# The tail of a graph-attention kernel: moments a slot sooner, scores ahead of the next product, two totals written together, the last quad whole

## The chip, the cores and the metric

The kernel runs on one core of one Trainium2 chip. The metric is the device time of an execution in microseconds (us); lower is better. Engines are named as in the profile: PE is TensorE (PEld its weight loads), DVE is VectorE, ACT is ScalarE, POOL is GpSimd, SP is SyncE, whose queue issues most DMAs. Before the change three runs took 2006.64, 2006.75 and 2006.97 us, a median of 2006.75.

## The reference, cut to what matters

A graph with 6250 nodes of 128 features and 206,250 edges, sorted by receiver. Each edge gets a weight vector from two small networks, a score per head (8 heads of 16), and a message; a node sums the messages that it receives, adds its own features and is normalized.

```
w     = silu(edge_a @ rad_W1 + b) @ rad_W2 + b  +  silu(edge_b @ sph_W1 + b) @ sph_W2 + b
alpha = sum over a head of (q[receiver] * w * k[sender]) / sqrt(16) * edge_weight
out   = segment_sum(alpha * v[sender], receiver) / 16
y     = layernorm(x + out)
```

Here q, k and v are the node features times Wq, Wk, Wv.

## The kernel before, in words

**Tiles.** 128 edges are a tile, 4 tiles a quad (512 edges), 4 quads a group (2048 edges). There are 403 quads in NG = 101 groups, numbered 0 to 100; the last group has three quads, which the tail calls a = 400, b = 402 and c = 401 (within a group the order of the quads is 0, 2, 1, 3). A first stage makes a table of k and v rows in DRAM. Then the loop runs over the groups, with four slots in each, one for a quad.

**One quad.** GpSimd gathers the k and v rows of its senders from the table, one gather for a tile (`gather`, line 127), into one of 16 buffers, 14 quads ahead of use. TensorE computes the first layers (`first_layers`, L472), ScalarE their silu (L502), TensorE the receivers' q at the edges by a one-hot product (`q_at_edges`, L481) and the weights w (`weigh`, L512 and L517). VectorE then does five steps: `multiply` (L526, q times k; needs the gather and L481), and in `scores` the product with w (L534), the sum over a head (L536), the scaling (L538), and in `messages` the product with v (L551). The messages are summed by TensorE into 32 rows a quad (`sum_quads`, L563).

**One group.** `part_sums` (L592) copies a group's sums out of PSUM on ScalarE. `sum_group` (L597, L599) places them, by one-hot matrices that `place` makes on VectorE (L586, L587), into a window of 128 nodes and adds what the window before left there; a copy on ScalarE (L601) gives the total `tot` of the group. `moments` (L613, L615, L616) adds the node features and computes mean and variance on VectorE; `roots` (L621) takes the square root on ScalarE; `normalize` computes a reciprocal and a shift on VectorE (L629, L631) and applies them on ScalarE (L635). `write_rows` (L647) writes a window's 128 rows (64 KB) to `out` from the SP queue. Windows of neighbouring groups overlap, so the later write to a row is the right one and a write to `out` waits for the one before it.

**Four groups at a time.** In the loop, `statistics` takes the moments of the group two before in slot 3, and normalizes when four groups are together. The last four, 97 to 100, are normalized in the tail, each by its own root and normalize: 97 first, then 98, 99 and 100.

**The tail** (lines 745 to 799). The three last quads have wide one-hots (`wide_one_hots`), so that `sum_wide` (L578) adds their messages straight into the last window, in PSUM, and `to_end` (L776) adds what group 99 left there. Before the change c is treated in two halves of two tiles: multiply, scores, messages and sums of a half, then of the other, with the normalize of 98 and the moments of 99 between them.

**The order of the work** is written out by hand: every engine runs its instructions in the order of the program, and semaphores are put in where one needs another's result. PSUM tiles have few buffers (`ph`, `pq`, `pw` two each, `po` one), so a product waits until the buffer's last reader is done. In the loop, `marks` are matmuls of the next quad's product: the helpers `after` and `behind` make an instruction on VectorE or ScalarE wait for one of them, so that it comes no sooner than this matmul; `mark` is the last matmul of `q_at_edges`.

Of the kernel before, what the change touches and what calls it, by code (L numbers as in the profile page):

```python
# [60 lines left out]
def gnn_kernel(ctx, tc, x, src, dst, weight, edges, rad_W1, rad_b1, rad_W2, rad_b2,  # L61
# [404 lines left out]
    with tc.tile_pool(name="ps", bufs=1, space=PSUM) as pp:  # L466
# [55 lines left out]
        def multiply(q, mark=None, t=slice(0, QT)):  # L522
            if t.start == 0:
                kq_of[q] = quad_of("kq", 3)
            for u, kv in kv_parts(q, t):
                o = nc.vector.tensor_tensor(kq_of[q][:, u, :], pq_of[q][:, u, :], kv[:, :, :D],  # L526
                                            op=OP.mult)
                if mark is not None:
                    after(o, mark)
# [15 lines left out]
        def messages(q, alpha, t=slice(0, QT), marks=()):  # L545

            if t.start == 0:
                msg_of[q] = quad_of("msg", XQ)
            for u, kv in kv_parts(q, t):
                n = u.stop - u.start  # L550
                o = nc.vector.tensor_tensor(  # L551
                    msg_of[q][:, u, :].rearrange("p t (h e) -> p t h e", e=HD),
                    kv[:, :, D:].rearrange("p t (h e) -> p t h e", e=HD),
                    alpha[:, u.start - t.start:u.stop - t.start, :, None].to_broadcast(
                        [P, n, HEADS, HD]), op=OP.mult)
                behind(o, marks, 3)
# [20 lines left out]
        def sum_wide(q, t, start=False, stop=False):  # L577
            nc.tensor.matmul(po_of[q // NQ], hot_of[q, "wide"][:, t, :], msg_of[q][:, t, :],  # L578
                             start=start, stop=stop)
# [9 lines left out]
        def part_sums(g):  # L589
            n = quads_in(g) * W  # L590
            part_of[g] = gp.tile([P, D], F32, name="part")
            nc.scalar.activation(part_of[g][:n, :], po_of[g][:n, :], AF.Copy)  # L592
# [46 lines left out]
        def statistics(g):  # L639
            moments(g, tot_of[g])  # L640
            if g < NG - LB and first_of(g + 1) > g:
                normalize(first_of(g), g + 1, roots(first_of(g), g + 1))
# [42 lines left out]
        for g in range(NG - 1):  # L685
            for slot, j in enumerate((0, 2, 1, 3)):
                q = g * NQ + j
                i = g * NQ + slot
                turned, past, old = None, mark, marks
                if slot == 0 and g == CHECK + len(checks) + 1:  # L690
                    verdict()
                if slot == 0:
                    turned = turn_q(g + 1, pp.tile([P, EQ], F32, name="pq", bufs=2))
                if slot == 1 and 2 <= g:
                    turned = sum_group(g - 2)
                if slot == 2:
                    turned = make_q(g + 1, pp.tile([P, EQ], F32, name="pq", bufs=2))
                if 1 <= g:
                    for t in ((), (0, 1), (2,), (3,))[slot]:
                        mark = sum_quads(g - 1, t)  # L700
                first_layers(order[i + 2])
                mark = q_at_edges(order[i + 1])
                marks = weigh(order[i + 1])
                silus(order[i + 2], mark, marks)
                if turned:
                    turned()
                if 1 <= g and slot == 3:
                    part_sums(g - 1)
                if i + AHEAD < len(order):
                    gathers(order[i + AHEAD], old[-QT:])  # L710
                multiply(order[i + 1], mark)
                messages(q, scores(q, marks=marks), marks=marks)
                if slot == 0:
                    if g + XL < NG:
                        load_x(g + XL, past)
                if slot == 2:
                    if g + 3 < NG:
                        load_feats(g + 3, past)
                    if g + 2 < NG:
                        load_rel(g + 2)  # L720
                if slot == 1:
                    one_hots_T(g + 1)
                    if g + 2 < NG:
                        pick(g + 2)
                    if 1 <= g:
                        place(g - 1)
                write_rows()
                load_rows(i)
                if slot == 3:
                    if 2 <= g:  # L730
                        statistics(g - 2)
                    if g + 1 < NG - 1:
                        one_hots(g + 1)
                    if CHECK <= g < CHECK + len(checks):
                        checks[g - CHECK]()
                if g == NG - 3 and slot in (0, 2):
                    wide_one_hots(order[slot // 2 - 3])
                if g == NG - 2 and slot == 0:
                    wide_one_hots(order[-1])
                    n = nc.values_load(general, min_val=0, max_val=1)  # L740
                if g == NG - 2 and slot == 2:
                    place(NG - 1)
                if g == NG - 2 and slot == 3:
                    place(g)
        g, (a, b, c) = NG - 1, order[-3:]
        halves = (slice(0, QT // 2), slice(QT // 2, QT))
# [1 line left out]
        mark = q_at_edges(b)  # L748
        marks = weigh(b)
        turned = sum_group(g - 2)  # L750
        for t in range(QT // 2):
            sum_quads(g - 1, t)
        silus(c, mark, marks)
        sd = roots(g - 3, g - 2)
        turned()
        multiply(b, mark)
        messages(a, scores(a, marks=marks), marks=marks)
        normalize(g - 3, g - 2, sd)
        write_rows()

        mark = q_at_edges(c)
        marks = weigh(c)
        for t in range(QT // 2, QT):
            sum_quads(g - 1, t)
        po_of[g] = pp.tile([P, EQ], F32, name="ph", bufs=2)[:, :D]
        for t in range(QT):
            sum_wide(a, t, start=(t == 0))
        part_sums(g - 1)
        turned = sum_group(g - 1)
        messages(b, scores(b, marks=marks), marks=marks)  # L770
        moments(g - 2, tot_of[g - 2])
        sd = roots(g - 2, g - 1)
        turned()
        for t in range(QT):
            sum_wide(b, t)
        nc.tensor.matmul(po_of[g], to_of[g][:, 1, :], tot_of[g - 1], start=False, stop=False)  # L776

        multiply(c, mark, halves[0])
        messages(c, scores(c, halves[0]), halves[0])
        for t in range(QT // 2):  # L780
            sum_wide(c, t)
        normalize(g - 2, g - 1, sd)
        write_rows()
        moments(g - 1, tot_of[g - 1])
        sd = roots(g - 1, g)
        multiply(c, mark, halves[1])
        messages(c, scores(c, halves[1]), halves[1])
        for t in range(QT // 2, QT):
            sum_wide(c, t, stop=(t == QT - 1))
        normalize(g - 1, g, sd)  # L790
        write_rows()
        moments(g, po_of[g])
        sd = roots(g, g + 1)
        rs = gp.tile([P, LB], F32, name="rs")
# [163 lines left out]
```

## Time and profile before

| | |
|---|---|
| median of three runs | 2006.75 us |
| profiled execution | 2007.43 us |
| its span, first to last instruction | 2005.3 us |
| PE busy | 1806.6 us (90%) |
| POOL busy | 1502.9 us (75%) |
| DVE busy | 1468.5 us (73%) |
| ACT busy | 718.5 us (36%) |
| last gather starts | 1987.24 us |
| last write of rows starts | 2000.85 us |

Times inside the profile are microseconds from the start of the span. The profiled execution took 2.13 us more than its span, and 0.68 us more than the median. A line of a view in order of time gives start, duration, engine, source line, operation, the tile written and the tiles read, shapes, and in brackets how long the engine sat idle before it and what ended that. VectorE starts an instruction a little before the one ahead of it has ended, so the steps between starts are what adds up. Busy time of PE counts overlapping matmuls and is not PE at its peak. A line of waits gives who waited, for whom, and then the total, the number of times and the longest.

The core's stages:

| us from the start | what runs | DVE busy |
|---|---|---|
| 0 to 55 | tables, node products, first gathers | 38.62 |
| 55 to 1988.2 | the loop and the start of the tail, gathers all along | 1420.19 |
| 1988.2 to 2000.85 | the rest of the tail | 9.67 |
| 2000.85 to 2005.3 | the last write and the end of the program | 0.00 |

### The profile page before, as it was taken

To read this page: it belongs to the slowest core of one execution; us is meant where nothing else is said; L and a number is where in the kernel's file an instruction comes from. 1 tells how busy PE (TensorE), PEld (TensorE's weight loads), DVE (VectorE), ACT (ScalarE), POOL (GpSimd) and SP (SyncE) were. 2 spreads that over 40 slices of the span, in tenths; PEclk is the share of its full clock that TensorE was granted. 3 is DMA by queue.
4 is the path that set the end of the run, shared out by engine and by line. 5 is a ranking of instruction groups with operands and counts; after the bars stand their busy time and mean duration, and the time that the engine had idled before them with its cause. 6 is when DMAs were issued, how large, how long until landed. Compare 5 with 4: busy or idle time off the path is not lost.

```text
span 2005.3 us, 51075 instructions
## 1 busy us (share of the span) xinstructions
PE 1806.6 (90%) x16012; PEld 1521.8 (76%) x16012; DVE 1468.5 (73%) x3087; ACT 718.5 (36%) x1426; POOL 1502.9 (75%) x1594
## 2 busy tenths in 40 slices
PE   9999999989899988989998899898988999888897
PEld 7788777867777767778877777777777777777776
DVE  6688787858787767777777676776767767767677
ACT  3244344424343333333333333342433333333333
POOL 7777777777777777777777777777777777777775
PEclk9899989988988988988888889898889888898898
DMA  8545555545555555555555555554455455455453
GB/s 313 158 141 153 149 150 152 157 142 153 154 144 152 155 144 153 154 144 151 155 145 153 147 147 152 144 156 140 141 155 154 143 150 156 142 151 144 139 154 86
DMA packets 146834, 304.50 MB, mean 152 GB/s; under 512 B 36940, under 2 KB 80060, under 8 KB 146556
## 3 DMA queue, kind: packets, MB, share of 16 engines
q0 software_dynamic: 75488, 205.36, 36.7%
q1 hardware_dynamic: 69568, 95.42, 14.6%
q8 instruction: 128, 2.10, 0.4%
q14 instruction: 150, 1.23, 0.2%
q10 hardware_dynamic: 1500, 0.40, 0.1%
HBM read 287.58 MB, written 13.46 MB: 150 GB/s over the span
## 4 chain that ended last, share of the span: by engine, by line
PE 61%; DMA 16%; DVE 9%; issue 5%; ACT 4%; POOL 3%; SPq 1%; DVEq 0%; POOLq 0%; ACTq 0%
PE pw L517 31%; DMA kv<-kv_tab,src_i 12%; PE pq L481 11%; PE ph L472 8%; PE po L563 4%; DVE kq L526 3%; DMA relb<-rel_lin 3%; PE pw L512 3%; POOL msg L127 2%; DVE kq L534 2%; ACT L502 2%; ACT y L635 1%; DVE side L536 1%; PE pq L212 1%; POOL kv L127 1%
## 5 line engine op out<-in xcount | busy, mean ns | idle before, releaser
L127 POOL DMA_INDIRECT kv<-kv_tab,src_i x1546 | 1463.0, 946 | 471.3 <-PE pw L517 182.9
L502 ACT ACTIVATE act<-ph,b 128x512 f32<-128x512 f32 x806 | 517.5, 685 | 1134.8 <-PE pq L481 1093.5
L517 PE MATMUL pw<-w,act 128*128 128x128 f32 x6448 | 914.8, 301 | 0.0
L517 PEld LDWEIGHTS pw<-w,act 128*128 128x128 f32 x6448 | 833.6, 209 | 105.8 <-issue 94.8
L481 PE MATMUL pq<-q,hotT 32*128 32x128 f32 x3224 | 505.5, 300 | 65.9 <-DVE hotT L218 43.0
L472 PE MATMUL ph<-feats,w 32*128 32x512 f32 x1612 | 502.3, 680 | 19.8 <-ACT act L502 19.0
L481 PEld LDWEIGHTS pq<-q,hotT 32*128 32x128 f32 x3224 | 424.8, 201 | 95.3 <-issue 57.7
L526 DVE TENSOR_TENSOR kq<-pq,kv 128x512 f32<-128x512 f32 (+1 forms) x404 | 273.8, 678 | 276.6 <-DMA kv<-kv_tab,src_i 122.2
L536 DVE TENSOR_REDUCE side<-kq 128x32 f32<-128x512 f32 x404 | 280.1, 693 | 42.8 <-DVE kq L534 0.9
L551 DVE TENSOR_TENSOR msg<-kv,side 128x512 f32<-128x512 f32 (+1 forms) x404 | 273.9, 678 | 42.9 <-DVE side L538 0.5
L534 DVE TENSOR_TENSOR kq<-pw,kq 128x512 f32<-128x512 f32 x404 | 274.5, 680 | 0.1
L472 PEld LDWEIGHTS ph<-feats,w 32*128 32x128 f32 x1612 | 136.8, 193 | 105.6 <-issue 60.5
L512 PE MATMUL pw<-brow,onesb 3*128 3x512 bf16 x403 | 162.5, 403 | 7.6 <-DVE kq L534 7.6
L563 PE MATMUL po<-msg,hot 128*32 128x128 f32 x3200 | 158.1, 295 | 0.0
L218 DVE TENSOR_TENSOR hotT<-relb,side 128x512 f32<-128x512 bf16 x101 | 68.9, 682 | 88.7 <-DMA relb<-rel_lin 88.7
L538 DVE TENSOR_TENSOR side<-side,scale 128x32 f32<-128x32 f32 x404 | 80.6, 200 | 42.6 <-DVE side L536 0.9
L597 PE MATMUL pq<-part,to 128*128 128x128 f32 x200 | 44.7, 307 | 68.9 <-DVE kq L526 46.7
L563 PEld LDWEIGHTS po<-msg,hot 128*32 128x32 f32 x3200 | 72.6, 113 | 39.6 <-issue 7.3
L597 PEld LDWEIGHTS pq<-part,to 128*128 128x128 f32 x200 | 31.8, 200 | 76.9 <-issue 43.9
L223 DVE TENSOR_TENSOR hot<-rel,side 128x512 f32<-128x512 f32 x100 | 66.2, 662 | 0.0
L212 PE MATMUL pq<-wq,xT 128*128 128x128 f32 x200 | 45.9, 316 | 18.6 <-DVE kq L526 18.5
L212 PEld LDWEIGHTS pq<-wq,xT 128*128 128x128 f32 x200 | 35.5, 222 | 21.8 <-DVE kq L526 21.4
(114 smaller groups left out, 849.6 us busy)
## 6 DMA issues: line engine op xcount, KB each, us to landing
wide<-kv_tab SPq DMA_DIRECT2D x3328, 1.0 KB
feats<-in_edges SPq DMA_DIRECT2D x101, 512.0 KB
kv<-kv_tab,src_i POOLq DMA_INDIRECT x1546
relb<-rel_lin SPq DMA_DIRECT2D x101, 128.0 KB
x<-in_x SPq DMA_DIRECT2D x101, 64.0 KB
out<-y SPq DMA_DIRECT2D x101, 64.0 KB
kv_tab<-kv SPq DMA_DIRECT2D x12, 512.0 KB
act<-in_x SPq DMA_DIRECT2D x12, 256.0 KB
```

Of the source, the lines that this page charges most:

```text
L127: return nc.gpsimd.indirect_dma_start(out=o, out_offset=None, in_=table, in_offset=bass.IndirectOffsetOnAxis(ap=index, axis=0))
L212: nc.tensor.matmul(pt[:n, :D], xT_of[g][:, :n], wq, start=True, stop=True)
L472: return nc.tensor.matmul(act_of[q, i], w1[r0:r0 + R, :], feats_of[g][r0:r0 + R, c0:c0 + EQ], start=True, stop=True)
L481: o = nc.tensor.matmul(pq_of[q][:, t, :], hotT_of[g][b, t * P:(t + 1) * P], q_of[g][b, :], start=True, stop=True)
L502: o = nc.scalar.activation(act, act_of[q, i], AF.Silu, bias=b1[:, i:i + 1])
L512: nc.tensor.matmul(pw, onesb, brow.rearrange("p t d -> p (t d)"), start=True, stop=False)
L517: o = nc.tensor.matmul(pw[:, t, :], act_of[q, i][:, t * P:(t + 1) * P], w2[:, i, :], start=False, stop=(t == QT - 1 and i == 1))
L526: o = nc.vector.tensor_tensor(kq_of[q][:, u, :], pq_of[q][:, u, :], kv[:, :, :D], op=OP.mult)
L534: nc.vector.tensor_tensor(m, pw_of[q][:, t, :], m, op=OP.mult)
L536: o = nc.vector.tensor_reduce(alpha, m.rearrange("p t (h e) -> p t h e", e=HD), AX.X, OP.add)
L551: o = nc.vector.tensor_tensor(msg_of[q][:, u, :].rearrange("p t (h e) -> p t h e", e=HD), kv[:, :, D:].rearrange("p t (h e) -> p t h e", e ...
L563: o = nc.tensor.matmul(po_of[g][j * W:(j + 1) * W, :], hot_of[g][:, j * QT + t, :], msg_of[g * NQ + j][:, t, :], start=(t == 0), stop=(t = ...
```

## The change

In the loop, `statistics` of group 97 and `place` of group 99 move from slot 3 of group 99 to slot 2. In the tail, a's scores and messages stand ahead of b's multiply, and the waits of scores and messages for `marks` are dropped; all of group 99's quads are summed in one place, its part is copied and its total summed ahead of c's product; the moments of 98 and 99 stand together, with one root and one normalize for both, and their rows are written one behind the other; c is multiplied and scored whole, and only its messages and their sums are in halves.

```diff
                 write_rows()
                 load_rows(i)
-                if slot == 3:
+                if slot == (3 if g < NG - 2 else 2):
                     if 2 <= g:
                         statistics(g - 2)
+                if slot == 3:
                     if g + 1 < NG - 1:
                         one_hots(g + 1)
...
                 if g == NG - 2 and slot == 2:
                     place(NG - 1)
-                if g == NG - 2 and slot == 3:
                     place(g)
...
         turned = sum_group(g - 2)
-        for t in range(QT // 2):
+        for t in range(QT):
             sum_quads(g - 1, t)
         silus(c, mark, marks)
         sd = roots(g - 3, g - 2)
         turned()
+        part_sums(g - 1)
+        messages(a, scores(a))
         multiply(b, mark)
-        messages(a, scores(a, marks=marks), marks=marks)
         normalize(g - 3, g - 2, sd)
         write_rows()
 
         mark = q_at_edges(c)
+        turned = sum_group(g - 1)
         marks = weigh(c)
-        for t in range(QT // 2, QT):
-            sum_quads(g - 1, t)
+        turned()
         po_of[g] = pp.tile([P, EQ], F32, name="ph", bufs=2)[:, :D]
         for t in range(QT):
             sum_wide(a, t, start=(t == 0))
-        part_sums(g - 1)
-        turned = sum_group(g - 1)
-        messages(b, scores(b, marks=marks), marks=marks)
-        moments(g - 2, tot_of[g - 2])
-        sd = roots(g - 2, g - 1)
-        turned()
+        nc.tensor.matmul(po_of[g], to_of[g][:, 1, :], tot_of[g - 1], start=False, stop=False)
+        messages(b, scores(b))
         for t in range(QT):
             sum_wide(b, t)
-        nc.tensor.matmul(po_of[g], to_of[g][:, 1, :], tot_of[g - 1], start=False, stop=False)
-
-        multiply(c, mark, halves[0])
-        messages(c, scores(c, halves[0]), halves[0])
-        for t in range(QT // 2):
-            sum_wide(c, t)
-        normalize(g - 2, g - 1, sd)
-        write_rows()
+        moments(g - 2, tot_of[g - 2])
         moments(g - 1, tot_of[g - 1])
-        sd = roots(g - 1, g)
-        multiply(c, mark, halves[1])
-        messages(c, scores(c, halves[1]), halves[1])
-        for t in range(QT // 2, QT):
-            sum_wide(c, t, stop=(t == QT - 1))
-        normalize(g - 1, g, sd)
-        write_rows()
+        sd = roots(g - 2, g)
+        multiply(c, mark)
+        normalize(g - 2, g, sd)
+        write_rows(2)
+        alpha = scores(c)
+        for h in halves:
+            messages(c, alpha[:, h], h)
+            for t in range(h.start, h.stop):
+                sum_wide(c, t, stop=(t == QT - 1))
         moments(g, po_of[g])
         sd = roots(g, g + 1)
```

## The prediction

> **What bounds the kernel now.** First view: the costliest groups of the page.
>
> ```profile
> L127 POOL DMA_INDIRECT kv<-kv_tab,src_i x1546 | 1463.0, 946 | 471.3 <-PE pw L517 182.9
> ```
>
> GpSimd issues 1546 gathers, each 0.946 us busy and 0.30 idle. 1546 x 1.25 = 1932 us, which is the whole stretch from the first kv gather to the last (1987.24). So up to about 1988 the gather queue sets the time, and the change leaves it alone: it can only alter what follows the last gathers. Second view: VectorE in order of time (start, duration, line, operation, tiles), from quad 397's messages to the end.
>
> ```profile
> 1979.30 0.69 DVE L551 TENSOR_TENSOR msg<-kv,side 128x512 f32<-128x512 f32 x1
> 1979.90 0.35 DVE L587 TENSOR_SCALAR to_end<-side,rowp 128x128 f32<-128x128 f32 x1
> 1980.41 0.69 DVE L526 TENSOR_TENSOR kq<-pq,kv 128x512 f32<-128x512 f32 x1 [0.16 <-PE pq L481]
> ...
> 1983.51 0.31 DVE L613 TENSOR_TENSOR y<-tot,x 128x128 f32<-128x128 f32 x1
> ...
> 1984.51 0.34 DVE L587 TENSOR_SCALAR to<-side,rowp 128x128 f32<-128x128 f32 x1
> 1985.60 0.69 DVE L526 TENSOR_TENSOR kq<-pq,kv 128x512 f32<-128x512 f32 x1 [0.75 <-DMA kv<-kv_tab,src_i]
> ...
> 1992.11 0.18 DVE L616 BATCH_NORM_AGGREGATE mv<-st 128x2 f32<-128x6 f32 x1
> 1992.21 0.41 DVE L526 TENSOR_TENSOR kq<-pq,kv 128x256 f32<-128x256 f32 x1
> ...
> 1995.23 0.40 DVE L526 TENSOR_TENSOR kq<-pq,kv 128x256 f32<-128x256 f32 x1
> ...
> 1996.80 0.42 DVE L551 TENSOR_TENSOR msg<-kv,side 128x256 f32<-128x256 f32 x1
> ...
> 1998.03 0.29 DVE L613 TENSOR_TENSOR y<-ph,x 128x128 f32<-128x128 f32 x1 [0.54 <-PE ph L578]
> ...
> 1999.48 0.35 DVE L798 TENSOR_SCALAR y<-y,mv,rs 128x128 f32<-128x128 f32 x1
> ```
>
> The reader is to see that VectorE waits once, 0.75 us for b's rows at 1985.60 (b = 402, c = 401, a = 400), and is then busy without a gap until c's second messages at 1996.80. The chain of waits puts 7.46 us on a gather before 1992.21, but that multiply starts 0.10 after the aggregate, as the one at 1995.23 does after its own: no wait. Third view: the last gather on GpSimd, the write queue, and its last long wait.
>
> ```profile
> 1987.24 0.95 POOL L127 DMA_INDIRECT kv<-kv_tab,src_i  x1 [0.30 <-issue]
> ...
> 1965.38 0.36 SPq L647 DMA_DIRECT2D out<-y  x1
> ...
> 1967.95 0.34 SPq L647 DMA_DIRECT2D out<-y  x1
> ...
> 1970.43 0.33 SPq L647 DMA_DIRECT2D out<-y  x1
> ...
> 1995.10 0.33 SPq L647 DMA_DIRECT2D out<-y  x1
> ...
> 1998.04 0.33 SPq L647 DMA_DIRECT2D out<-y  x1
> 2000.85 0.34 SPq L799 DMA_DIRECT2D out<-y  x1
> ```
>
> ```profile
> SPq L799 <- DMA out<-y: 2.4, 1, 2.4
> ```
>
> A write to out waits for the one before it. The last rows are ready at 1999.83 (1999.48 + 0.35), but their write starts at 2000.85, 2.81 after the write of group 99. From there 4.45 us follow to the end of the span.
>
> **The change part by part.** Steps on VectorE, start to start, from this execution: multiply 0.61; L534 0.79, L536 0.80, L538 0.30, L551 0.60 (one quad's scores and messages: 2.49); a group's moments 0.33 + 0.33 + 0.10 = 0.76; place 0.25 to 0.27 an instruction; reciprocal 0.19 and shift 0.08.
>
> *Moments of 97 and place of 99, a slot sooner.* Three and two VectorE instructions, no DMA (97 is not normalized there), no SP or GpSimd work. Their input, tot of 97, was copied by ScalarE at 1972.76, so they run at once. Messages of 397 at 1979.30, moments 1979.90, place(100) 1980.66, place(99) 1980.93 and 1981.20, multiply(a) 1981.45 instead of 1980.41. Behind multiply(a) on VectorE, L534 of 399 goes from 1981.02 to 1982.06; TensorE needs its buffer for the product of b (L512, 1983.43), so 0.7 us remain. The gathers no longer wait for this. In slot 3 the 1.3 us are missing, so b's rows (landed about 1985.5) would be waited for: the next part fills that.
>
> *Scores of a ahead of multiply(b).* L534(399) 1982.06, messages(399) 1983.95, L534(a) 1984.55 (its product was done at 1982.53), messages(a) 1986.44, multiply(b) 1987.04: no idle. The dropped waits for TensorE cost nothing seen: with them L536(a) followed L534(a) by 0.78, the same step as everywhere; I take 0, with 0.07 either way (the longest "issue" piece of this chain on VectorE).
> The price is that multiply(b) comes 1.44 later, and c's q at the edges waits for it on TensorE, with the sum of 99, c's product and the wide sums of a and b queued behind. L481 started 0.74 after such a multiply at 1960.16, so 1987.78; L481 to L517 takes 1.09 (1986.73 to 1987.82), the sum of 99 0.65 (1985.51 to 1986.16): c's product from 1989.52 to 1991.57.
>
> *All four sums of 99's quads at once.* The second sixteen matmuls, 0.57 to 0.65, run at 1986.7, needing messages(399) (done 1984.6). TensorE is idle from about 1987.3 to 1987.78. The copy of the part (0.28 on ScalarE) is then early; tot of 99 is copied near 1989.8, behind normalize(97) on ScalarE (shift 1987.84, done 1988.5). It used to land at 1992.8.
>
> *Both moments, one root, one normalize.* From multiply(b) 1987.04: reciprocal 1987.65, shift 1987.84, L534(b) 1987.92, messages(b) 1989.81, moments of 98 at 1990.41 and 99 at 1991.17, multiply(c) 1991.93. One root for two columns instead of two (ScalarE 0.29 less; 128x1 takes 0.294, 128x4 0.30). It is done about 1992.36, while multiply(c) runs: reciprocal 1992.54, shift 1992.73, L534(c) 1992.81, 1.2 us after c's product.
>
> *Last quad whole.* c's halves took 1.99 + 1.91 = 3.90; whole it takes 0.61 + 0.79 + 0.80 + 0.30 + 2 x 0.34 = 3.18. Six VectorE instructions fewer, 0.72 saved. Messages at 1994.70 and 1995.04. Then 1.23 to the last y (1996.80 to 1998.03), or up to 1.35 because eight matmuls run in a row (1.06 to 1.16 against 0.71 for four): I take 1.30, y at 1996.34. From y 1.80 to the end of L798: rows ready at 1998.14 instead of 1999.83, a gain of 1.69.
>
> *Two writes in a row.* The first copy by ScalarE (L635) starts 0.20 after shift and takes 0.49: rows of 98 at 1993.42, of 99 at 1993.8 (four in a row took 1.65). Write of 98 at 1993.45, write of 99 when that has landed, the last when 99 has. Back-to-back spacings in the trace: 2.57, 2.48 (two) and 2.81. I take 2.48 for the first and 2.81 for the second, which is the same pair at the same place: last write at 1998.74, 0.6 after its rows. Ends: 2 x 2.81 gives 1999.07; no wait gives 1998.17.
>
> Sum: last write from 2000.85 to 1998.74, 2.11 us sooner; ends 1.78 and 2.68. The 4.45 behind it stays. Against the profiled execution (span 2005.3, time 2007.43) that is 2005.3. The median of the runs shown is 0.68 below it, so I forecast 2006.75 - 2.11 = 2004.64.
>
> **A rule against the rows.** The Trainium skill, "DMA: Bandwidth & Descriptors", section "Anatomy of one DMA", has a fixed cost of about 2.0 us a DMA, most of it the write's receipt, plus bytes over 436 GB/s. By it 64 KB would take an estimated 2.15 us, two in a row would be over before the last rows are ready, and the time would be 2004.07. The row of 2.81, which holds issue, landing and wake-up, speaks for the longer one.
>
> **The rivals.**
> 1. *The writes don't bind.* If a write frees the next 2.3 us or less after its issue, the last write starts with its rows at 1998.17: gain 2.68, time 2004.07. For it: other waits of SP for out ended sooner after the issue (1.2 us). Against: all four back-to-back spacings are above 2.3. This is how the rule above would have it.
> 2. *TensorE's clock halves.* After idle gaps of 2.1 and 1.1 us (1964.04 to 1968.56) the granted clock was 0.50 from 1968.2 to 1974.7, and the sixteen matmuls of a product took 3.5 instead of 1.9. If that happened at 1987.78, c's product would end near 1994.4, L534(c) and all behind 1.6 later, the last write about 1999.8: gain 1.05, time 2005.7. Against: the gap there is 0.5 us.
> 3. *The gathers hold c.* Multiply(c) moves to 1991.93. The last gather starts at 1987.24; rows of earlier quads were there 2.7 to 3.2 us after the start, so 1990.5. Landing would have to take 4.7 us before it costs anything; at 5 us, the longest wait of multiply on a gather being 5.3, and the gain falls to 1.8: 2004.9.
> 4. *The other side: the write chain.* The change puts two landings ahead of the last write, starting at 1993.45, where before only that of 99, issued at 1998.04, lay at the end. At a spacing above 3.70 us (1993.45 + 2 x 3.70 = 2000.85) the kernel is slower than before; at 4.2 it takes 2007.75, and 0.2% slower takes 5.7. For it: the last wait was the longest in the tail. Against: no spacing above 2.81, and little other traffic after 1990 (mean 20 to 30 GB/s).
> 5. *It gains nothing* (2006.75): the order on VectorE would have to wait as much as it saves, for instance for tot of 99 (1.4 us to spare) or c's product (1.2).
>
> **How the numbers follow.** My sum 0.58, rival 1 0.20, rival 2 0.06, rival 3 0.06, rival 4 0.04, rival 5 0.06. The likeliest is 2004.64, with 2004.1 to 2005.0 of its own. For eight in ten I add about 0.5 below rival 1 for the landing of the last write (the queue waited 1.3 us for it), and above I reach past rival 2: 2003.6 to 2006.1. 0.2%, about 4.0 us, is what a measurement of this kernel can tell from no change. All but the extreme of rival 4 lie inside it; faster by 4.0 would need the last write at 1996.8, only 0.5 after the last y: 0.04. Slower by 4.0: 0.03, with what I have not thought of.
>
> **What would show it.** In the changed kernel's trace: L613 and L616 ahead of multiply(a), at about 1980; no wait for kv at b's multiply, about 1987.0; multiply(c) 128x512 near 1991.9; messages 128x256 twice within 0.4 us near 1995; two L647 writes 2.5 apart; L798 about 1997.8; L799's write within 0.6 us of its end. Wrong if the last gather shifts by more than 0.5 us, if VectorE waits for tensor work at L613 or L534, if the clock shows 0.50 near 1990, or if L799's wait is over 1 us.

## The result and the profile after

| | before | after |
|---|---|---|
| median of 18 runs each, one chip | 2006.94 us (2006.17 to 2008.00) | 2002.80 us (2002.29 to 2003.61) |
| ratio | | 0.998 (95%: 0.9972 to 0.9987) |
| profiled execution, its span | 2007.43, 2005.3 us | 2002.76, 2000.9 us |
| last gather starts | 1987.24 us | 1986.14 us |
| last rows ready | 1999.83 us | 1997.11 us |
| last write starts | 2000.85 us | 1997.14 us |
| last write to the end of the span | 4.45 us | 3.76 us |

The kernel gained 4.14 us, or 0.2%: little, but the interval of the ratio lies clear of 1. It is nearly twice the 2.11 us that I forecast. The time of 2002.80 us lies below the low end of my range (2003.6).

The page's costliest group is the same as before, as it should be: 1546 gathers, 0.946 us each.

```profile
L127 POOL DMA_INDIRECT kv<-kv_tab,src_i x1546 | 1462.4, 946 | 471.2 <-issue 192.6
```

VectorE of the changed kernel in order of time, from quad 397's messages to the end (start, duration, line, operation, tiles, idle time before it):

```profile
1978.86 0.69 DVE L551 TENSOR_TENSOR msg<-kv,side 128x512 f32<-128x512 f32 x1
1979.46 0.28 DVE L613 TENSOR_TENSOR y<-tot,x 128x128 f32<-128x128 f32 x1
...
1980.96 0.68 DVE L526 TENSOR_TENSOR kq<-pq,kv 128x512 f32<-128x512 f32 x1
...
1984.05 0.69 DVE L534 TENSOR_TENSOR kq<-pw,kq 128x512 f32<-128x512 f32 x1
1984.77 0.69 DVE L536 TENSOR_REDUCE side<-kq 128x32 f32<-128x512 f32 x1
1985.50 0.20 DVE L538 TENSOR_TENSOR side<-side,scale 128x32 f32<-128x32 f32 x1
1985.74 0.69 DVE L551 TENSOR_TENSOR msg<-kv,side 128x512 f32<-128x512 f32 x1
1986.34 0.68 DVE L526 TENSOR_TENSOR kq<-pq,kv 128x512 f32<-128x512 f32 x1
...
1991.08 0.69 DVE L526 TENSOR_TENSOR kq<-pq,kv 128x512 f32<-128x512 f32 x1
...
1993.64 0.75 DVE L551 TENSOR_TENSOR msg<-kv,side 128x256 f32<-128x256 f32 x2
1995.31 0.29 DVE L613 TENSOR_TENSOR y<-ph,x 128x128 f32<-128x128 f32 x1 [0.92 <-PE ph L578]
...
1996.77 0.34 DVE L790 TENSOR_SCALAR y<-y,mv,rs 128x128 f32<-128x128 f32 x1
```

The order is the forecast one, and from the messages of 397 to those of c no instruction shows idle time: the wait for b's rows, 0.75 us before the change, is gone. The steps inside a quad are new. L534 of a to L536 takes 0.72, on to L538 0.73, on to L551 0.24. The same quad before the change, where the steps are 0.78, 0.80 and 0.31 (0.79, 0.80 and 0.30 in most quads of the loop):

```profile
1986.21 0.68 DVE L534 TENSOR_TENSOR kq<-pw,kq 128x512 f32<-128x512 f32 x1
1986.99 0.69 DVE L536 TENSOR_REDUCE side<-kq 128x32 f32<-128x512 f32 x1
1987.79 0.20 DVE L538 TENSOR_TENSOR side<-side,scale 128x32 f32<-128x32 f32 x1
1988.10 0.69 DVE L551 TENSOR_TENSOR msg<-kv,side 128x512 f32<-128x512 f32 x1
```

The writes of rows on the SP queue, the last three of the changed kernel, and then what SP's last write waited for (total, times, longest):

```profile
1992.60 0.33 SPq L647 DMA_DIRECT2D out<-y  x1
...
1994.23 0.33 SPq L647 DMA_DIRECT2D out<-y  x1
...
1997.14 0.34 SPq L791 DMA_DIRECT2D out<-y  x1
```

```profile
SPq L791 <- DMA out<-y: 1.2, 1, 1.2
```

The two writes that now follow each other are 1.63 us apart, and the last one starts 0.03 after its rows: 1996.77 + 0.34 = 1997.11. It waits 1.2 for a landing, but that is over before the rows are there: at the same spacing of 1.63 it would end at 1995.86.

Where the 4.67 us between the two profiled executions (2007.43 and 2002.76) went:

| piece | before | after | gained | forecast |
|---|---|---|---|---|
| start to the messages of 397 | 1979.30 | 1978.86 | 0.44 | 0 |
| from there until the last rows are ready | 20.53 | 18.25 | 2.28 | 1.69 |
| rows ready to last write | 1.02 | 0.03 | 0.99 | 0.42 |
| last write to the end of the span | 4.45 | 3.76 | 0.69 | 0 |
| outside the span | 2.13 | 1.86 | 0.27 | 0 |

The first piece isn't the change's: it varies by some 3 us between executions of the same kernel (below).

### The profile page after: what moved, and what is told of

Its sections match the earlier page's. It is cut to its first block, busy times and chain, and to the rows that moved or that the text cites. A ratio compares the mean times of both kernels' runs of the same rounds, so it can differ in the third digit from the quotient of the medians.

```text
span 2000.9 us, 51060 instructions
## 1 busy us (share of the span) xinstructions
PE 1798.5 (90%) x16012; PEld 1515.2 (76%) x16012; DVE 1469.0 (73%) x3081; ACT 718.2 (36%) x1425; POOL 1501.9 (75%) x1594
## 3 DMA queue, kind: packets, MB, share of 16 engines
q14 instruction: 150, 1.23, 0.2%
## 4 chain that ended last, share of the span: by engine, by line
PE 57%; DMA 17%; DVE 10%; issue 6%; SPq 4%; ACT 3%; POOL 3%; DVEq 0%; ACTq 0%; POOLq 0%
PE pw L517 29%; DMA kv<-kv_tab,src_i 13%; PE pq L481 10%; PE ph L472 7%; PE po L563 4%; DVE kq L526 4%; PE pw L512 3%; SPq L167 3%; DMA relb<-rel_lin 2%; POOL msg L127 2%; DVE kq L534 2%; PE pq L212 1%; DVE side L536 1%; POOL kv L127 1%; ACT L502 1%
## 5 line engine op out<-in xcount | busy, mean ns | idle before, releaser
L536 DVE TENSOR_REDUCE side<-kq 128x32 f32<-128x512 f32 x403 | 280.1, 695 | 42.6 <-DVE kq L534 0.9
L551 DVE TENSOR_TENSOR msg<-kv,side 128x512 f32<-128x512 f32 (+1 forms) x404 | 273.9, 678 | 42.8 <-PE pw L517 0.9
L534 DVE TENSOR_TENSOR kq<-pw,kq 128x512 f32<-128x512 f32 x403 | 274.7, 682 | 0.0
L538 DVE TENSOR_TENSOR side<-side,scale 128x32 f32<-128x32 f32 x403 | 80.6, 200 | 42.4 <-DVE side L536 0.9
```

What stands on the lines that cost most here:

```text
L534: nc.vector.tensor_tensor(m, pw_of[q][:, t, :], m, op=OP.mult)
L536: o = nc.vector.tensor_reduce(alpha, m.rearrange("p t (h e) -> p t h e", e=HD), AX.X, OP.add)
L551: o = nc.vector.tensor_tensor(msg_of[q][:, u, :].rearrange("p t (h e) -> p t h e", e=HD), kv[:, :, D:].rearrange("p t (h e) -> p t h e", e ...
```

## The experiments

Several of the chips on which they ran granted TensorE 0.81 to 0.83 of its full clock instead of 0.91 to 0.92, so that the whole program took 2620 to 2650 us there and single executions differ by 10 us and more; of those runs the tail in the trace is read first. Its measure is the *stretch*, from the start of quad 397's messages to the start of the last write: 21.55 us before the change and 18.28 after it.

### 1. The slot

```diff
-                if slot == (3 if g < NG - 2 else 2):
+                if slot == 3:
                     if 2 <= g:
                         statistics(g - 2)
-                if slot == 3:
...
                     place(NG - 1)
+                if g == NG - 2 and slot == 3:
                     place(g)
```

> The changed kernel with the moments of 97 and place(99) put back into slot 3. Chain theory (VectorE is busy without a gap from quad 397's messages to c's messages, so only idle time that a step fills is won): multiply(a) comes about 1.0 us sooner, as soon as its q product is there, but 1.27 us of moments and place follow before a's scores; L534 of a about 0.3 us later than in the changed kernel, time 0.3 us above it, 2003.1 (gain against before 3.8). Rival (moving these five instructions is what brought the gain): 1.3 us above it, 2004.1 or more.

VectorE of this kernel from the messages of 397:

```profile
2617.63 0.69 DVE L551 TENSOR_TENSOR msg<-kv,side 128x512 f32<-128x512 f32 x1
...
2618.74 0.69 DVE L526 TENSOR_TENSOR kq<-pq,kv 128x512 f32<-128x512 f32 x1 [0.16 <-PE pq L481]
```

The stretch is 18.53: 0.25 more than after. A little of that is seen here: the multiply of a waits 0.16 for TensorE's product, which the moved work covers when it stands there. By the trace the slot by itself is worth a quarter of a microsecond, on a chip whose gathers had ended some 45 us before. The time was 2646.26 against 2650.65 before (ratio 0.9985, 0.9970 to 0.9999).

I then moved the same work one slot further:

```diff
-                if slot == (3 if g < NG - 2 else 2):
+                if slot == (3 if g < NG - 2 else 1):
...
-                if g == NG - 2 and slot == 2:
+                if g == NG - 2 and slot == 1:
                     place(NG - 1)
                     place(g)
```

> The changed kernel with the moments of 97 and both place steps in slot 1 of group 99, where VectorE waits 1.77 us for TensorE. Chain theory: multiply(a) comes as soon as its q product is there, 1.0 us sooner, with nothing to make up for later; from quad 397's messages to the last write 17.3 us instead of 18.28, if b's and c's rows are there by then; 2001.8. Rival (the gathered rows of b or c bind as soon as VectorE is earlier): less than 0.4 us won, 2002.5.

The stretch fell to 17.46 in that trace, 0.82 less. There the multiply of a starts 0.99 us after the messages of 397 (2.10 after the change) with 0.30 of waiting for TensorE, and a new wait of 0.19 for the root of 97 stands at L629. The time did not show it: 2621.93 against 2622.07 before (0.9975 to 1.0011), on a chip whose executions ran from 2616 to 2632 us.

### 2. The order of a's scores and b's multiply

```diff
-        messages(a, scores(a))
         multiply(b, mark)
+        messages(a, scores(a))
```

It was run three times, since on the first two chips the last gather had started some 50 us before the messages of 397 and could hold nothing.

> The changed kernel with b's multiply ahead of a's scores again. Chain theory: the multiply waits for b's gathered rows, which land 3.2 us after their last gather starts; 0.3 to 1.0 us of idle on VectorE, and that much more time, 2003.1 to 2003.8. Rival (the gathered rows of b are there in any case, or TensorE's earlier q of c makes up for it): within 0.1 us of the changed kernel, 2002.8.

> The changed kernel with b's multiply ahead of a's scores, where the gathers bound the loop. Chain theory: VectorE waits for b's rows before that multiply, 0.3 to 1.0 us, and the stretch from quad 397's messages to the last write grows from 18.28 to 18.6 to 19.3 us. Rival: b's rows are there, 18.28.

> The changed kernel with b's multiply ahead of a's scores, once more, for a run in which the gathers bound the loop. Chain theory: where the last gather of b starts less than 4 us before that multiply could, VectorE waits for it and the stretch from quad 397's messages to the last write is 18.6 to 19.3 us; where the gathers are long done, 18.28. Rival: 18.28 in any case.

Where the gathers are early the stretch stays at 18.28, twice, so the order costs nothing by itself. (The times: 2648.80 against 2650.65, ratio 0.9971 to 0.9997, on the first, and single executions of 2630.38 and 2003.47 on the others.) On the third chip, where the gathers last until the tail, it is 19.57, 1.29 more. VectorE of that run, the messages ahead of b's multiply and the multiply, and then the last gather on GpSimd:

```profile
1983.26 0.69 DVE L551 TENSOR_TENSOR msg<-kv,side 128x512 f32<-128x512 f32 x1
1985.10 0.69 DVE L526 TENSOR_TENSOR kq<-pq,kv 128x512 f32<-128x512 f32 x1 [1.15 <-PE pw L517]
```

```profile
1986.74 0.94 POOL L127 DMA_INDIRECT kv<-kv_tab,src_i  x1 [0.30 <-PE po L563]
```

VectorE idles 1.15 us. The line names TensorE, but the same order waited for nothing on the other chips. What differs is the gathers: the last gather of b, four before the last of all, starts at 1981.75, and the multiply comes 3.35 after it. In the kernel before, where the wait is put down to the gather, it came 3.36 after (1982.24 to 1985.60). That the wait is for gathered rows is inferred from this agreement. By it the reorder fills such a wait, and only where the gathers are the bound. Even there the wait is not in every execution: in a profile of the kernel before with its last code left out (third run in experiment 6) the multiply of b comes 3.51 after that gather (1981.44 to 1984.95) and waits for nothing.

### 3. The waits that were dropped

I put waits back on a's and b's L536, L538 and L551, on matmuls that are done by then:

```diff
-        for t in range(QT):
-            sum_quads(g - 1, t)
+        late = [sum_quads(g - 1, t) for t in range(QT)]
...
-        messages(a, scores(a))
+        messages(a, scores(a, marks=marks), marks=marks)
...
-        messages(b, scores(b))
+        messages(b, scores(b, marks=late), marks=late)
```

> The changed kernel with the six waits of a's and b's L536, L538 and L551 for TensorE put back, on matmuls that are done long before, so that nothing is really waited for. Theory (a second wait on a VectorE instruction costs time of its own): the steps of a and b go from 0.72, 0.73, 0.24 back to 0.79, 0.80, 0.30, so 0.40 us in all, time 2003.2. Rival (the steps are shorter in the tail because other engines are quieter): steps stay at 0.72, 0.73, 0.24 and the time at 2002.8.

> Once more the changed kernel with the six waits back, timed where medians repeat. Theory (0.07 us a wait, on the path): 0.4 us above the changed kernel, 2003.2, 3.7 us below the kernel before. Rival (hidden behind gathered rows or TensorE): 2002.8, 4.1 below.

VectorE of the second of these runs, quad a and the start of b:

```profile
1987.11 0.68 DVE L534 TENSOR_TENSOR kq<-pw,kq 128x512 f32<-128x512 f32 x1
1987.90 0.69 DVE L536 TENSOR_REDUCE side<-kq 128x32 f32<-128x512 f32 x1
1988.70 0.20 DVE L538 TENSOR_TENSOR side<-side,scale 128x32 f32<-128x32 f32 x1
1989.00 0.69 DVE L551 TENSOR_TENSOR msg<-kv,side 128x512 f32<-128x512 f32 x1
1989.61 0.68 DVE L526 TENSOR_TENSOR kq<-pq,kv 128x512 f32<-128x512 f32 x1
```

The steps are back at 0.79, 0.80 and 0.30, though no idle time is shown and the matmuls waited for were done. In the same trace c, which kept no such wait, stays at 0.72, 0.73 and 0.23. The stretch is 18.70 in the first run and 18.69 in the second: 0.41 more for six waits, 0.07 each. The time of the first was 2646.40 against 2650.65 (0.9969 to 0.9997). The time of the second was 2005.51 against 2008.99, a gain of 3.48 (ratio 0.9982, 0.9973 to 0.9991), where the change alone gained 4.14 on its own chip. A run on a third chip gave the same steps, at 2650.40 against 2650.66 (0.9987 to 1.0011):

> The changed kernel with the six waits of a's and b's scores and messages back, where the gathers bound the loop. Theory (each second wait on a VectorE instruction costs 0.07 us): stretch from quad 397's messages to the last write 18.70 us instead of 18.28, time 0.4 us above the changed kernel, 2003.2. Rival (b's or c's rows or TensorE bind, so that 0.4 us on VectorE is hidden): 2002.8.

### 4. The quad c in halves

```diff
-        multiply(c, mark)
+        multiply(c, mark, halves[0])
         normalize(g - 2, g, sd)
         write_rows(2)
-        alpha = scores(c)
         for h in halves:
-            messages(c, alpha[:, h], h)
+            if h.start:
+                multiply(c, mark, h)
+            messages(c, scores(c, h), h)
```

> The changed kernel with c multiplied and scored in two halves again, the normalize of 98 and 99 behind the first multiply. Chain theory: the halves take 1.91 each against 2.90 whole (0.61, 0.72, 0.73, 0.24, and 0.34 for each half's messages less what runs together), so c's second messages come 0.7 to 0.9 us later and the time is 2003.6. Rival (the first half's wide sums run earlier, TensorE has half as many behind the second, and that pays for it): within 0.3 us of the changed kernel.

The stretch is 18.96: 0.68 more, where I had worked out 0.72 for taking c whole, less 0.07 for its longer wide sums. That the two agree is partly luck: my 0.72 set halves, which never carried the waits of experiment 3, against a whole c whose steps did. Without those waits c whole takes 2.98 on VectorE and the halves of this run 3.84, which is 0.86; 0.10 of it is lost in the longer wide sums and 0.09 in a later multiply. The time was 2649.74 against 2650.66 (0.9984 to 1.0010).

### 5. The chain of writes

Is it 2.5 to 2.8 us from write to write, as the four spacings before had it? Here the two writes stand behind c's messages, so that three follow each other at the end:

```diff
         multiply(c, mark)
-        normalize(g - 2, g, sd)
-        write_rows(2)
         alpha = scores(c)
         for h in halves:
             messages(c, alpha[:, h], h)
             for t in range(h.start, h.stop):
                 sum_wide(c, t, stop=(t == QT - 1))
+        normalize(g - 2, g, sd)
+        write_rows(2)
```

> The changed kernel with the normalize of 98 and 99 behind c's messages, so that three writes to out stand in a row at the end. It measures what a write ahead of the last one costs there. If a write frees the next 1.63 us after its issue, as the two in the changed kernel's tail: writes at about 1994.9, 1996.6 and 1998.2 against 1997.14 in the changed kernel, 1.0 us above it, 2003.8. If 2.5 to 2.8, as in the loop and at the end of the kernel before: 3.0 us or more above it, 2005.8 or more.

The writes on SP, the wait of the last one, and the DMA queues in two stretches of this run, 2650.5 to 2651.5 and 2651.5 to 2652.5 (packets, MB, share of the 16 engines):

```profile
2647.79 0.33 SPq L647 DMA_DIRECT2D out<-y  x1
...
2650.15 0.33 SPq L647 DMA_DIRECT2D out<-y  x1
...
2653.21 0.34 SPq L791 DMA_DIRECT2D out<-y  x1
```

```profile
SPq L791 <- DMA out<-y: 2.7, 1, 2.7
```

```profile
q1 hardware_dynamic: 135, 0.06, 20.9%
q8 instruction: 1, 0.02, 6.5%
q14 instruction: 1, 0.01, 2.7%
...
q1 hardware_dynamic: 8, 0.00, 2.6%
```

The spacings are 2.36 and 3.06, and the last write starts 3.52 after its rows (2649.34 + 0.35 = 2649.69). The time was 2650.07 against 2650.65 (0.9974 to 1.0007). So a write can hold the next one for 3 us after all, and the queues say when. A write is 144 packets. Here 135 go together, two instruction packets pass in the same time, and the others come one by one in the microsecond and a half behind. In the kernel before it was the same, its last nine packets passing between 1999.6 and 2000.2: the DMA queues from 1998.7 to 1999.4, in the write that made the last one wait, which was issued at 1998.04:

```profile
q1 hardware_dynamic: 135, 0.06, 29.9%
q8 instruction: 1, 0.02, 8.3%
```

In the changed kernel all 144 packets of the write at 1992.60 pass between 1992.9 and 1994.3 with no instruction packet among them:

```profile
q1 hardware_dynamic: 144, 0.07, 15.9%
```

So the long spacings at the end go with the fetching of program code. That this delays the stragglers is inferred from the two standing together, in these two traces. A packet that passes only behind the 144, as one did after the write at 1994.23, held nothing up: SP's wait was over after 1.63.

The kernel before, profiled once more on another chip:

> The kernel before, unchanged, profiled once more, to see what of its last 7 us is the same each time. Theory (packets of instruction fetch fall on one of the 16 DMA engines while the write of group 99 is under way, because the engines reach the end of their instructions there): the write of 99 again has 8 or 9 of its 144 packets late, the last write again starts 2.4 to 2.9 us after it, and about 4.4 us follow. Rival (the 2.81 us were chance): spacing of the two writes 1.8, last write as soon as its rows are ready, 3.2 to 3.8 us behind it.

Its write of 99 again has an instruction packet ahead of it and nine packets behind the other 135, but SP's wait for it was 1.9 and not 2.4. The last two writes are 2.33 apart (2609.04 and 2611.37), and the last one starts 0.04 after its rows: nothing is lost to the write. Its rows came later behind the write of 99 instead, 2.29 and not 1.79. The four wide sums of c's second half, which waited 2.23 for VectorE, took 1.22 and not 0.71, at a granted clock of 0.50 to 0.57. So the 0.99 that the profiled pair gains at the write is not in every execution of the kernel before; in this one, 0.51 of it sat in TensorE.

### 6. The code behind the tail

The instruction packets led to the last term that I had held fixed. Behind the tail stands the code for receivers that lie outside the windows, which does not run here. These kernels leave out the body of it:

```diff
-        with tc.For_i(0, NG, 1) as g:
-            general_group(g)
-        with tc.For_i(0, N - P, P) as r:
-            general_rows(r)
-        general_rows(N - P)
```

In the kernel before:

> The kernel before without the two loops of the general path behind the tail (they don't run on these data; what is left out is the code that would treat receivers outside the windows). Theory (instruction fetch for what lies behind the tail holds the writes): fewer instruction packets in the last 7 us, the last write as soon as its rows are ready, 1.0 us sooner, and 3.2 us behind it instead of 4.45; 2.2 us faster than before, 2004.7. Rival (the writes are slow there for another reason): spacing stays at 2.4 to 2.8 and the time within 0.3 us of before.

> The kernel before without the loops of the general path, timed where the gathers bound the loop. Theory (instruction packets hold the last writes): at least the 1.8 us behind the last write that the trace showed, and up to 1.0 more where the last write waited; 2004.1 to 2005.1. Rival (they overlap with something else that ends the program): within 0.3 us of before, 2006.9.

> Once more the kernel before without the loops of the general path, for a chip on which the gathers bound the loop and medians repeat within 0.5 us. Theory (instruction packets hold the last writes and the end): 1.8 us or more below the kernel before. Rival (cutting the code moves as much time elsewhere in the program, as the two timings on slower chips suggest, which showed no gain within 2 us): within 0.5 us of the kernel before.

And in the changed one:

> The changed kernel without the two loops of the general path (which don't run on these data). Theory: nothing to win at the last write, which doesn't wait, but 2.7 us behind it instead of 3.5 to 3.8; 2001.8, 1.0 us below the changed kernel, so that the difference to the kernel before, cut in the same way, is 3.3 us or less instead of 4.1. Rival: 2002.8.

> Once more the changed kernel without the loops of the general path, beside the other. Theory: 2.7 us behind the last write instead of 3.5 to 3.8, so 0.8 to 1.1 us below the changed kernel (2001.8), and 2.3 to 3.3 us below the kernel before cut in the same way: the change on VectorE (2.3) without what the instruction packets add. Rival: the same 4.1 us apart.

| cut | clock | last write to end of span, us | median, us | before there, us | ratio (95%) |
|---|---|---|---|---|---|
| before, first | 0.82 | 2.69 | 2623.57 | 2622.07 | 1.0001 (0.9985 to 1.0017) |
| before, second | 0.82 | 2.64 | 2651.31 | 2650.66 | 1.0008 (0.9997 to 1.0019) |
| before, third | 0.91 | 2.72 | 2006.71 | 2008.99 | 0.9991 (0.9982 to 1.0000) |
| after, first | 0.81 | 2.71 | 2645.91 | 2650.66 | 0.9988 (0.9976 to 0.9999) |
| after, second | 0.92 | 2.65 | 2004.52 | 2008.99 | 0.9978 (0.9969 to 0.9987) |

The DMA queues of the cut kernel before (third run) from its second-last write to the end, with no instruction queue in the list, and what its last write waited for:

```profile
q1 hardware_dynamic: 288, 0.13, 7.8%
```

```profile
SPq L799 <- DMA out<-y: 1.2, 1, 1.2
...
SPq L799 <- DVE y L798: 0.7, 1, 0.7
```

Two whole writes and nothing else, a wait of 1.2 that is over in time, and then the wait for the rows. Against 4.45 and 4.53 with that code, the end of the span comes 2.64 to 2.72 after the last write, in all five cut kernels. On the chip at 0.91 of the clock the kernel before gains 2.28 us by medians from the cut alone, more than the whole of what I forecast for the change, though the interval of the ratio just reaches 1. At the lower clock no gain is seen, and in the second run a gain of 2 us is outside the interval; why is open.

On that chip the two cut kernels are 2.19 us apart (2006.71 and 2004.52). That is the change without the program's end, and close to the 2.28 of VectorE's piece; I expected 2.3 to 3.3. In their traces the stretches are 20.59 and 18.27. But the nearness is in part chance, since the cut kernel before differs from the kernel before in its tail as well:

```profile
1989.47 0.69 DVE L536 TENSOR_REDUCE side<-kq 128x32 f32<-128x512 f32 x1 [0.48 <-PE pw L517]
```

All three of its traces have this wait of b's L536 for TensorE, which neither profile of the uncut kernel has, and about 0.51 more in slow wide matmuls; none has the 0.75 for b's rows. Why leaving out code behind the tail brings this wait is open. The cut of the changed kernel was expected to gain 0.8 to 1.1 over the change alone. It gained 4.47 against 4.14, on different chips. On its own chip the changed kernel with the six waits took 2005.51; less their 0.41 that is an estimate of 2005.10 for the changed kernel there, 0.58 above the cut one.

### 7. A version meant to be better

Experiment 1's further slot, with the normalize of 97 moved behind b's messages, so that the root is no longer waited for:

```diff
         messages(a, scores(a))
         multiply(b, mark)
-        normalize(g - 3, g - 2, sd)
-        write_rows()
...
         for t in range(QT):
             sum_wide(b, t)
+        normalize(g - 3, g - 2, sd)
+        write_rows()
```

> The slot 1 version (moments of 97 and both place steps in slot 1 of group 99), with the normalize of 97 moved behind b's messages, where its square root is surely there (in the slot 1 version VectorE waited 0.19 us for it). Chain theory: from quad 397's messages to the last write 17.2 us, against 18.28 in the changed kernel and 17.46 in the slot 1 version; where the gathers bound the loop 1.0 us less than the changed kernel, 2001.8, if b's rows are there. Rival (gathered rows of b or c bind): VectorE waits for kv at b's or c's multiply and the stretch is 17.8 or more.

> The changed kernel once more, to see what of its end repeats. Theory (instruction packets fall on the same writes each time): the writes of 98 and 99 1.63 apart, the last one as soon as its rows are ready, 18.3 us from quad 397's messages, 3.5 to 3.8 us behind it. Rival (chance): the spacing or the stretch behind the last write differs by more than 0.4 us.

It took 2002.90 (2002.25 to 2006.58) against 2006.86, a gain of 3.96: no better than the change. In its profiled execution, the one of 2006.58, the stretch is 18.07 and not the 17.46 of the further slot alone. The multiply of a waits 0.89, put down to TensorE, and starts 2.90 after a's last gather (1980.47). On this chip the gathers end with the tail, and what is done sooner on VectorE ends up waiting. That those 0.89 are the gathered rows was not isolated.

The changed kernel itself, profiled there, took 2006.45 in that one execution: messages of 397 at 1981.98, last gather at 1990.26, against 1978.86 and 1986.14 in the first. Its stretch is 18.32, its two writes are 1.64 apart, and the last starts with its rows, but 4.40 follow it and not 3.76 (4.94 in the execution of 2006.58). So the stretch repeats within 0.04 us; its start moves by 3 us with the gathers, and what follows the last write is not the same every time.

## Why the prediction was wrong, step by step

**Right.** Up to about 1988 the gathers set the time: nothing ahead of the tail moved that another execution doesn't move as much. The moved slot is worth little by itself (0.25). The reorder is what takes away the wait for b (1.29 us when undone, in the one trace in which the gathers bind). No idle time is left on VectorE between 397's and c's messages. Taking c whole saves 0.68 (0.72 less 0.07 worked out, partly by luck, as said in experiment 4). From c's first messages to y it took 1.67 (forecast 1.64), with the eight wide matmuls in a row at full clock. The rivals of the clock, the held c and the slow write chain did not come about.

**"The dropped waits cost nothing seen ... I take 0."** This failed. I reasoned that L536 followed L534 by the same 0.78 as everywhere, but every 128x512 L536 in that trace carried such a wait. It costs 0.07 us even when what it waits for is over. Six of them are 0.41 (experiment 3). My 3.18 for c also used steps with waits, where 0.07 + 0.07 + 0.06 = 0.20 goes too. Together 0.61, which is the whole difference between 1.69 and 2.28 in that piece, within 0.02; the other differences, of at most 0.1 each, cancel. The bound of 0.07 that I gave for all six was what one of them costs.

**"I take 2.48 for the first and 2.81 for the second."** This failed too. The first was 1.63 and the second no wait; rival 1, to which I gave 0.20, was right on the writes. The four spacings that I read were three from the time when the gathers' traffic ran and one with an instruction packet in it, and I took them for the write's own duration. (That the gathers' traffic lengthened the first three was not tested.) The row I set against them (SP's other waits for out, 1.2 us) was the better one. The Trainium skill's rule in "DMA: Bandwidth & Descriptors", "Anatomy of one DMA" (about 2.0 us plus the bytes, an estimated 2.15 here), was on the same side, and by it the time would have been 2004.07. The section gives it for DMAs that GpSimd issues, and these writes are SP's; the undisturbed write freed the next in 1.63, less than the rule has. The spacings of 2.36 to 3.06 in experiment 5 are above it.

**"The 4.45 behind it stays."** This was never checked: I took what follows the last write as a constant of the kernel. It is 3.76 in the profiled execution, 4.40 in another of the same kernel, 3.19 to 3.78 in the variants of it in experiments 1 to 5, 4.94 in that of experiment 7, and 2.64 to 2.72 with the code behind the tail left out. So 1.7 to 1.9 of the 4.45 and 4.53 go with that code being there. Where the 0.69 of the profiled pair went is seen in what SP's queue waits for at the program's end, first before and then after the change:

```profile
SPq L955 <- DMA out<-y: 1.3, 1, 1.3
...
SPq L947 <- DMA out<-y: 0.7, 1, 0.7
```

SP waits 0.6 less for the last write's landing, most of the 0.69. In the two longer ends of 4.40 and 4.94 its wait for TensorE's queue is the one that grew, from 0.7 to 1.6 and 2.3. Why these waits vary is open.

**Outside the span.** I took this as fixed as well. It is 1.78 on average over the 18 runs of the changed kernel, and 1.96 to 2.01 on each chip for the kernel before. The cut kernels before have 1.77 to 1.78, with nothing else edited, and the cut changed ones 1.77 and 1.80. So these 0.2 us go with the code behind the tail in the kernel before, but not in the changed one; how is open.

By medians: 2.11 forecast, 0.61 for the waits, 0.57 for the writes (2.68, the end I gave for no wait, less 2.11), 0.69 behind the last write and about 0.2 outside the span make 4.2, against 4.14. Two of these terms are held by a profiled pair alone. The 0.57 has to be read with the second profile of before, which lost nothing at the write but 0.51 at TensorE's clock. The 0.69 would be 0.13 by the other pair (4.53 and 4.40). The part of VectorE is settled, then, and the division of the other two microseconds is not; that they come from the program's end is supported by the two cut kernels, which differ by 2.19 only, but not shown, since the cut also brought a wait into the tail of one of them.

## What to carry to other kernels

When a change removes a wait that is always fulfilled, look for an instruction of the same kind without one before calling it free; and size a step from rows that carry the same waits as the new one will. A spacing read from a trace is only a duration if the queues show nothing else in it: list the DMA queues, instruction packets too, over that stretch. At a change of 0.1 to 0.2%, what follows the last write and what lies outside the span are terms of the sum like the others, and even code that never runs can be worth as much as was forecast for the edit.

## What the runs showed of the hardware that I had not expected

- A wait that is over costs 0.06 to 0.07 us on VectorE: steps of 0.79, 0.80 and 0.30 with it, 0.72, 0.73 and 0.24 without, in one and the same trace.
- Code behind the tail that doesn't run puts instruction packets beside the last writes. Without it the end of the span is 1.7 to 1.9 us nearer to the last write in the kernel before, and 0.5 to 1.7 nearer in the changed one (3.19 to 4.40 in it and its variants of experiments 1 to 5, against 2.65 and 2.71).
- TensorE's clock halved within a gap of 2.23 us in which VectorE worked, in four of five traces of the kernel before and of its cuts (the four matmuls behind it took 1.22 to 1.23). The matmuls of the cut kernel before (third run) show it, and then its table of windows (busy time of PE, PEld, DVE, ACT and POOL, then the granted clock, the DMA share and GB/s):

```profile
1996.98 1.23 PE L578 MATMUL ph<-msg,wide 128*128 128x128 f32 x4 [2.23 <-DVE msg L551]
```

```profile
1996.00:1997.00 1.00, 0.02 (x1) 0.02 (x1) 0.93 (x4) 0.00 (x0) 0.00 (x0) 0.79 0.00 0
1997.00:1998.00 1.00, 1.00 (x4) 0.91 (x4) 0.16 (x2) 0.49 (x1) 0.00 (x0) 0.50 0.00 0
```

In the fifth trace, the profiled execution of before, the same four took 0.71 behind the same gap, and the clock fell only afterwards (0.91 from 1998 to 1999, then 0.50). In the changed kernel the eight wide matmuls of c took 1.16 in every trace in which c is whole, behind gaps of 0.58 to 2.56 us. A gap's length alone doesn't tell, then. The Trainium skill, "TensorE: Matmul & The Clock Gate", Part 1, has a free-running window of about 3.4 us that must be idle; that the length alone doesn't decide agrees with a free-running window, but a fall within 2.23 us of idling is sooner than its figure.
